# Interleaved query projections, a narrower last sampling tile and moved maxima in a four-layer image network

## The chip, the cores and the metric

The kernel runs on one core of one Trainium2 chip, as one launch. The metric is the device time of that launch in microseconds (us). A core has a matmul engine (TensorE; PE in the profile, its weight loads PEld), a vector engine (VectorE; DVE), a scalar engine (ScalarE; ACT), GpSimd (POOL) and a queue that issues transfers (SP). Each takes its own list of instructions in order, and they wait for each other by semaphores. All arithmetic here is in 32-bit floats.

## The reference

Two images of 512 channels and 64 x 64 pixels go through four layers, each of the form `x = x + layer(groupnorm(x))`. Layer 0 is an attention over local and pooled keys, layer 3 a linear attention. The change is in layer 1 and in the passage to layer 2. Cut to these:

```python
def gn(v, G=32): ...                                   # mean and variance over groups of 16 channels

def layer1(x):                                         # deformable attention
    q = einsum('oc,bchw->bohw', w_q, x)                # 512 x 4096 queries per image
    oi = q.reshape(b * 8, 64, 64, 64)                  # 8 heads of 64 channels
    off = tanh(w_off2 @ gelu(oi[:, :, ::4, ::4] * w_off1 + b_off1)) * 4.0
    grid = (16 x 16 grid points + off), scaled to the image
    kv_feats = grid_sample_bilinear(oi, grid)          # 256 points per head, sampled from q
    k, v = split(w_kv @ kv_feats)
    out = softmax((q * 64 ** -0.5) @ k) @ v            # per head, 4096 queries, 256 keys
    return w_out @ out + b_out

def layer2(x):                                         # mixture of maximum pools
    s = relu(w2 @ relu(w1 @ mean(x) + b1) + b2)        # one number per channel
    pools = [maxpool_same(x, k) for k in (1, 3, 5, 7, 9, 11, 13)]
    lower = clip(floor(s), 0, 5)
    return (s - lower) * pools[lower + 1] + (lower + 1 - s) * pools[lower] + x
```

The maximum pools are made from each other: a 3 x 3 maximum of the 3 x 3 maximum is the 5 x 5 one, and so on. The first (3 x 3) is the "maxima" of this document.

## The kernel before, in words

An image lies in on-chip memory as a tile `X` of 128 partitions x 4 chunks x 4096 pixels (a chunk is 128 channels); a second one, `Y`, holds the queries and later the pools. The pixels are cut into 8 blocks of 512 (8 rows), and each block into 4 tiles of 128 pixels. The whole program runs twice, once per image. A scheduler orders each engine's instructions when the program is built, by the order of the source, by what is ready in its own model and by hand-written restrictions such as `issue_after`; on the chip that order is fixed.

**Queries and sampling** (`query_and_sample`). `query(blk)` makes one block's queries: for each of 4 chunks, 4 matmuls of 128 x 512 (line 134) into a bank of PSUM, then a ScalarE eviction into `Y` (line 1264), and after the four a VectorE maximum over the block (line 1267). Sampling is a matmul: for each pixel tile `t`, ScalarE and VectorE make the interpolation weights of 128 pixels against the grid points of 8 heads (lines 1297 to 1299, tile `wt`, two buffers); the matmul engine turns the tile's queries so that pixels lie on partitions (4 transposes, line 1302), ScalarE copies them out (line 1305, `q_tok`, two buffers), and 8 matmuls (line 1308), one per head, add into four accumulator banks `acc`. Only grid points near the pixels can have a weight: `keys_near(t)` gives the range of grid rows, 5 to 9 of 16. The first and the last tile take all 16 rows (256 columns), and they open and close the accumulation. The outer loop makes `query(blk + 1)` and then the four tiles of `blk`; the last block has no query to make. Then line 1310 copies `acc` into `feats`, and keys and values (lines 1064 and 1070) are made from that.

**Attention and the maxima** (`layer1`). A pipelined loop over 32 steps (block, chunk): line 1440 scores, 1443 exponentials (ScalarE), 1446 their sums over two key halves (GpSimd), 1455 weighted values, 1457 eviction; per block 1465 and 1471 inverse sums (VectorE reciprocal), 1479 and 1482 division, and, some steps later, one output chunk per step: `add_output`, 4 matmuls (line 1195), a VectorE eviction into `X` (line 1198) and statistics (line 1200). When a block's output is complete, `maxima_across` (lines 1132 and 1134 on VectorE, 1131 and 1133 on ScalarE for the two halo rows and the two edge columns) takes the maximum over three columns into `rows3`, a buffer of ten rows per chunk, and `maxima_down` (lines 1145 and 1146, and 1148 for the image's last row) that over three rows, into `Y`. Blocks 0 to 6 do this for four chunks at once (2048 elements per instruction). The last block does `maxima_across` chunk by chunk, `maxima_down` for chunk 0 next, and for chunks 1 to 3 after the mixture.

**The mixture** (`pool_mixture`). After the last block's statistics (line 1114, one per chunk) a chain of small matmuls and vector operations gives the group norm and the mixture's weights per channel, from line 1157 to line 1188. Line 1187 gives the weights; the instruction returned is line 1188, and `issue_after` holds everything under it behind that instruction.

**Layer 2** (`pool_chunk`). Per chunk of 128 channels, 7 weighted sources are added up in the 8 PSUM banks as matmuls with a diagonal matrix (line 1356, 8 per source; the diagonals are made on ScalarE, line 1361, in two buffers). Sources 0 and 1 are `X` and the maxima; each of the other five is made from the one before by two VectorE maxima over a whole image chunk (line 698), with edge copies on ScalarE (line 699). Then ScalarE evicts the chunk and squares it for statistics (lines 1398 and 1402).

Of the kernel before, what the change touches and what calls it, by code (L numbers as in the profile page):

```python
# [12 lines left out]
ALU = mybir.AluOpType  # L13
# [5 lines left out]
KC = C // P  # L19
# [3 lines left out]
NB = N // TB  # L23
# [3 lines left out]
NK = 256  # L27
# [23 lines left out]
def in_turn(*gens):  # L51


    gens = list(gens)
    while gens:
        gens = [g for g in gens if next(g, gens) is not gens]
# [877 lines left out]
class Net(General):  # L934
# [102 lines left out]
    def layer1(self, X, Y, d):  # L1037

        tc, nc, vec = self.tc, self.nc, self.vec
        with tc.tile_pool(name="l1", bufs=1) as sp:  # L1040
            wkv = sp.tile([P, KC, 2 * C], F32, name="wkv1")
            nc.sync.dma_start(wkv, d["w_kv1"].rearrange("(kc p) o -> p kc o", p=P))
            wq = sp.tile([P, KC, C], F32, name="wq1")
            feats = sp.tile([P, KC, NK], F32, name="feats")
            bq = sp.tile([P, KC], F32, name="bq1")
            with tc.tile_pool(name="l1a", bufs=1) as wp, \
                    tc.tile_pool(name="l1p", bufs=4, space=PSUM) as pp, \
                    tc.tile_pool(name="l1k", bufs=1, space=PSUM) as ppk:
                grid = wp.tile([P, 2, NK], F32, name="grid")
                nc.sync.dma_start(grid, d["grid"])  # L1050
                top = sp.tile([P, KC, NB], F32, name="top_q")
                self.query_and_sample(X, Y, wq, bq, grid, feats, top, wp, pp, ppk)
            self.ahead = ExitStack()
            dp = self.ahead.enter_context(tc.tile_pool(name="diags", bufs=1, side="right"))
            self.diags = cycle([dp.tile([P, P], F32, name=f"diag{i}") for i in range(2)])
            with tc.tile_pool(name="l1c", bufs=1) as late:

                keys = late.tile([P, KC, NK], F32, name="keys")
                vals = late.tile([P, 2, C], F32, name="vals")
                with tc.tile_pool(name="l1q", bufs=4, space=PSUM) as pp:  # L1060
                    for oc in range(KC):
                        ps = pp.tile([P, TB], F32, name="mm")
                        for kc in range(KC):
                            nc.tensor.matmul(ps[:, :NK], wkv[:, kc, oc * P:(oc + 1) * P],
                                             feats[:, kc, :], start=(kc == 0), stop=(kc == KC - 1))
                        nc.scalar.mul(keys[:, oc, :], ps[:, :NK], HD ** -0.5)
                    for t in range(2):
                        ps = pp.tile([P, TB], F32, name="mm")
                        for kc in range(KC):
                            nc.tensor.matmul(ps, feats[:, kc, t * P:(t + 1) * P], wkv[:, kc, C:],  # L1070
                                             start=(kc == 0), stop=(kc == KC - 1))
                        nc.vector.tensor_copy(vals[:, t, :], ps)
                    self.product_bound(top, keys, sp, pp)
                with tc.tile_pool(name="l1b", bufs=2) as wp, \
                        tc.tile_pool(name="l1s", bufs=6, space=PSUM) as pp, \
                        tc.tile_pool(name="l1o", bufs=2, space=PSUM) as ppo:
                    st = wp.tile([P, KC, NB, 6], F32, name="gn_st1", bufs=1)
                    w1 = wp.tile([P, KC, 32], F32, name="w1", bufs=1)
                    nc.sync.dma_start(w1, d["w1"].rearrange("(kc p) e -> p kc e", p=P))
                    w2 = wp.tile([32, C], F32, name="w2", bufs=1)  # L1080
                    nc.sync.dma_start(w2, d["w2"])
                    wo = wp.tile([P, KC, C], F32, name="wo1", bufs=1)
                    nc.sync.dma_start(wo, d["w_out1"].rearrange("(kc p) o -> p kc o", p=P))
                    steps = [(blk, cc) for blk in range(NB) for cc in range(KC)]
                    part = lambda blk, cc=slice(0, KC): Y[:, cc, blk * TB:(blk + 1) * TB]
                    flat = lambda a: a.rearrange("p k o -> p (k o)")
                    probs, totals, later = {}, {}, []
                    rows3 = flat(wkv)[:, :KC * 10 * W].rearrange("p (k y x) -> p k y x", k=KC, x=W)
                    ring = cycle([a[:, n:n + TB] for a, lo, hi in (
                        (flat(wq), 0, KC), (flat(wkv), 5, 8), (flat(feats), 0, 2),  # L1090
                        (wp.tile([P, 3 * TB], F32, name="totals", bufs=1), 0, 3))
                        for n in range(lo * TB, hi * TB, TB)]).__next__
                    for i in range(len(steps) + 4 + KC):
                        if i < len(steps):
                            blk, cc = steps[i]
                            probs[i], totals[i] = self.exponentials(part(blk, cc), keys[:, cc, :],
                                                                    ring, wp, pp)
                        if 1 <= i <= len(steps):
                            blk, cc = steps[i - 1]
                            self.attended(part(blk, cc), probs.pop(i - 1),  # L1100
                                          vals[:, :, cc * P:(cc + 1) * P], ppo)
                        at = lambda n: i >= n and (i - n) % KC == KC - 1 and (i - n) // KC
                        if (blk := at(1)) is not False and blk < NB:
                            r = self.inverse_sums([totals.pop(KC * blk + n) for n in range(KC)], wp,
                                                  pp)
                        if (blk := at(2)) is not False and blk < NB:
                            self.divided(part(blk), r, pp)
                        if (blk := at(3)) is not False and blk < NB:
                            later += [(blk, oc) for oc in range(KC)]
                        if later:  # L1110
                            blk, oc = later.pop(0)
                            self.add_output(X, wo, part(blk), blk, oc, st, pp)
                            if blk == NB - 1:
                                nc.vector.bn_aggr(self.mv[:, oc, :],
                                                  st[:, oc].rearrange("p b s -> p (b s)"))
                                self.maxima_across(X, blk, rows3, slice(oc, oc + 1))
                            elif oc == KC - 1:
                                self.maxima_across(X, blk, rows3, slice(0, KC))
                                self.maxima_down(Y, blk, rows3, slice(0, KC))
                    self.maxima_down(Y, NB - 1, rows3, slice(0, 1))  # L1120
                    with tc.issue_after(self.pool_mixture(w1, w2, wp, pp)):
                        self.maxima_down(Y, NB - 1, rows3, slice(1, KC))

    def maxima_across(self, X, blk, h, ks):

# [24 lines left out]
    def pool_mixture(self, w1, w2, sp, pp):  # L1150

        nc, vec, mv = self.nc, self.vec, self.mv
        c0, d0, wts = self.mix[:, 7], self.mix[:, 8], self.mix[:, :7]
        new = lambda name, n=1: sp.tile([P, n, KC], F32, name=f"pool_{name}", bufs=1)
        nmean, cent, var, rstd = (new(n)[:, 0] for n in ("nmean", "cent", "var", "rstd"))
# [3 lines left out]
        nc.vector.tensor_tensor(cent, mv[:, :, 0], ps[:, :KC], ALU.subtract)  # L1159
        nc.vector.tensor_tensor(var, cent, cent, ALU.mult)  # L1160
        nc.vector.tensor_tensor(var, var, mv[:, :, 1], ALU.add)
        ps = pp.tile([P, TB], F32, name="mm")
        nc.tensor.matmul(ps[:, :KC], self.grp, var, start=True, stop=True)
        nc.vector.tensor_scalar(var, ps[:, :KC], 1e-5, None, ALU.add)
# [20 lines left out]
        nc.vector.tensor_tensor(up, up, down, ALU.min)  # L1185
        nc.vector.tensor_scalar(up[:, :5], up[:, :5], 0.0, None, ALU.max)
        nc.vector.tensor_tensor(wts, up, bcast(rstd, 1, 7), ALU.mult)
        return nc.vector.scalar_tensor_tensor(c0, wts[:, 0], 1.0, rstd, ALU.add, ALU.add).ins

    def add_output(self, X, w, att, blk, oc, st, pp):  # L1190

# [57 lines left out]
    def query_and_sample(self, X, Y, wq, bq, grid, feats, top, wp, pp, ppk):  # L1249
# [3 lines left out]
        nc = self.nc  # L1253
# [31 lines left out]
            nc.gpsimd.tensor_copy(wq[:, kc], w[:, kc])  # L1285
        in_turn(self.grid_steps(banks, bq, grid, ycoord, hatx, wp, pp), query(0))
        for blk in range(NB):
            if blk + 1 < NB:
                in_turn(query(blk + 1))
            for t in range(blk * NT, (blk + 1) * NT):  # L1290

                near = self.keys_near(t) if 0 < t < n_t - 1 else slice(0, 16)
                some = lambda a: a.rearrange("p g (i j) -> p g i j", j=16)[:, :, :, near]
                wt = wp.tile([P, NH, NK], F32, name="wt", bufs=2)
                nw = NK // 16 * (near.stop - near.start)
# [10 lines left out]
                for g in range(NH):  # L1306
                    cc, lo = g // 2, (g % 2) * HD
                    nc.tensor.matmul(some(acc[:, :, :NK])[lo:lo + HD, cc], q[:, g * HD:(g + 1) * HD],
                                     wt[:, g], start=(t == 0), stop=(t == n_t - 1))
        nc.vector.tensor_copy(feats, acc[:, :, :NK])  # L1310

    def keys_near(self, t):

# [1496 lines left out]
```

## Time and profile before

| what | us |
|---|---|
| median of three runs | 5074.23 (5073.88 to 5079.57) |
| the profiled execution | 5069.52 |
| span of that execution, first to last instruction | 5067.7 |
| mean granted matmul clock | 0.984 of full |
| PE idle ahead of L1308 and L1064 at the end of the sampling, first image | 3.54 and 1.32 |
| PE idle ahead of L1157, both images | 7.26 each |
| L698, one maximum over an image chunk | 4.29 |
| L1356, the products of one source after the clock has risen | 6.86 from one to the next |

A line of the timeline gives the start in us from the span's start, the duration, the engine, the line of the kernel, the operation, output and inputs with shapes, and how many records were merged; a bracket gives the engine's idle time before, and who ended it. One 128 x 512 matmul of 32-bit floats leaves two records. Busy time of the engines in five stretches of the first image (us, then busy time with the number of records; the last columns are the matmul clock granted, the share of the transfer engines and GB/s):

```profile
core 0: us, PE busy (x) PEld busy (x) DVE busy (x) ACT busy (x) POOL busy (x), PEclk, DMA share, GB/s
1188.90:1222.90 34.00, 25.75 (x189) 15.82 (x187) 18.25 (x18) 14.44 (x19) 0.00 (x0) 0.90 0.01 2
1471.00:1498.20 27.20, 27.20 (x84) 10.53 (x82) 22.78 (x24) 3.31 (x11) 2.50 (x2) 1.00 0.00 0
1498.20:1514.40 16.20, 3.65 (x21) 3.28 (x20) 11.27 (x32) 1.56 (x6) 1.02 (x1) 0.62 0.00 2
1514.40:1568.60 54.20, 50.99 (x113) 22.18 (x114) 52.88 (x15) 13.47 (x40) 0.00 (x0) 0.96 0.11 39
1568.60:1715.00 146.40, 145.28 (x341) 63.91 (x339) 130.47 (x64) 49.08 (x135) 0.85 (x1) 1.00 0.00 0
```

The first stretch is the end of the sampling, the second the last block of the attention, the third the mixture, the fourth layer 2's first chunk, the fifth its other chunks. The fourth is the one in which VectorE is busier than the matmul engine.

### The profile page before, as it was taken

The numbers are of one execution on the slowest core, as the hardware profiler recorded it, in microseconds if no ns is written. First come the engines' busy times: TensorE is split into PE (matmuls) and PEld (weight loads), VectorE is DVE, ScalarE is ACT, GpSimd is POOL, SyncE is SP. The second block draws the span as 40 slices with busy tenths as digits, with TensorE's granted clock in tenths as the row PEclk, the third lists the DMA queues.
The fourth block names the chain that finished last, engine by engine and source line by source line (L and its number), as shares of the span: only waits on it lengthen the run. The fifth ranks groups of instructions, "written<-read, shape, count | busy, mean of one in ns | idle before, by whom it ended". The sixth has DMA issues, their size and how long they took to land. (4 is left out here: it accounts for less than half of the span.)

```text
span 5067.7 us, 48015 instructions
## 1 busy us (share of the span) xinstructions
PE 4822.0 (95%) x17027; PEld 1989.3 (39%) x17027; DVE 3069.5 (61%) x4010; ACT 1818.0 (36%) x3479; POOL 1848.2 (36%) x1218
## 2 busy tenths in 40 slices
PE   7999999999999999999999999999999999999998
PEld 3423332554334444433344233335543344444333
DVE  4266777754679533477732677777536794334776
ACT  1245555334323233321112555552443232333221
POOL 0035666501320145454500456664013201454554
PEclk9999999999999999999999999999999999999999
DMA  3035556600000000211110355565000000000111
GB/s 152 3 82 141 149 146 176 166 19 10 1 3 14 2 1 1 71 55 46 63 65 3 96 139 150 147 178 148 19 10 1 17 1 1 1 1 24 40 45 44
DMA packets 124172, 307.72 MB, mean 61 GB/s; under 512 B 20818, under 2 KB 33618, under 8 KB 122388
## 3 DMA queue, kind: packets, MB, share of 16 engines
q1 hardware_dynamic: 123924, 304.58, 20.8%
q8 instruction: 136, 2.23, 0.2%
q14 instruction: 112, 0.92, 0.1%
HBM read 256.01 MB, written 48.50 MB: 60 GB/s over the span
## 5 line engine op out<-in xcount | busy, mean ns | idle before, releaser
L134 PE MATMUL mm<-big,w 128*128 128x512 f32 x2496 | 1179.5, 616 | 32.3 <-DVE big L2404 9.5
L134 PEld LDWEIGHTS mm<-big,w 128*128 128x128 f32 x2496 | 458.5, 193 | 716.9 <-issue 558.8
L2613 POOL TENSOR_TENSOR late<-late,big 128x1024 f32<-128x1024 f32 x194 | 459.9, 2371 | 228.8 <-DVE big L2608 199.9
L2447 DVE TENSOR_TENSOR prods<-qs,big 128x1024 f32<-128x1024 f32 (+1 forms) x216 | 335.4, 1570 | 66.4 <-PE tap L2474 56.2
L1643 POOL TENSOR_TENSOR big<-big 128x512 f32<-128x512 f32 x224 | 277.6, 1272 | 219.3 <-ACT big L1634 219.3
L2608 DVE TENSOR_TENSOR big<-big,mm 128x512 f32<-128x512 f32 x388 | 254.6, 681 | 114.7 <-ACT mm L2600 113.3
L2600 ACT COPY mm<-big 128x512 f32<-128x512 f32 x432 | 247.4, 596 | 123.7 <-DMA big<-rows 78.2
L1634 ACT ACTIVATE big<-mm,ed 128x256 f32<-128x256 f32 x512 | 193.6, 489 | 233.1 <-DVE top L1630 200.4
L2518 POOL TENSOR_TENSOR late<-late 128x512 f32<-128x512 f32 x92 | 115.4, 1275 | 439.2 <-ACT late L2503 415.3
L2613 POOL TENSOR_TENSOR late<-late,tap 128x1024 f32<-128x1024 f32 x94 | 221.9, 2361 | 106.5 <-DVE tap L2608 93.6
L1446 POOL TENSOR_TENSOR wq<-prob 128x512 f32<-128x512 f32 x48 | 70.8, 1497 | 501.9 <-ACT prob L1443 501.9
L1898 PE MATMUL mm<-k,w 128*128 128x512 f32 x512 | 238.4, 609 | 12.3 <-DVE k L1891 7.3
L1630 DVE TENSOR_REDUCE top<-mm 128x1 f32<-128x512 f32 x256 | 159.0, 683 | 148.2 <-PE mm L1561 148.2
L1608 PE MATMUL mm<-w,big 128*128 128x512 f32 x512 | 235.3, 603 | 0.0
L134 PE MATMUL mm<-big,wq 128*128 128x512 f32 x512 | 232.4, 603 | 2.7 <-ACT off_t L1223 2.7
L1195 PE MATMUL mm<-big,wo 128*128 128x512 f32 x512 | 234.7, 604 | 0.0
L1356 PE MATMUL acc<-big,diag 128*128 128x512 f32 x512 | 227.3, 601 | 4.6 <-ACT diag L1361 4.6
L973 POOL TENSOR_TENSOR group_stats<-group_stats,cst 128x1 f32<-128x1 f32 (+1 forms) x20 | 12.1, 621 | 560.3 <-DVE group_stats L972 500.1
L1888 DVE RECIPROCAL psD<-psD 128x512 f32<-128x512 f32 x64 | 215.1, 3361 | 1.9
L134 PE MATMUL mm<-big,big 128*128 128x512 f32 x464 | 201.7, 594 | 0.5 <-DVE b_sr L1011 0.5
L2474 PE MATMUL tap<-prods,cst 128*32 128x512 f32 x1152 | 193.1, 604 | 4.8 <-DVE prods L2447 4.3
L1443 ACT ACTIVATE prob<-mm 128x512 f32<-128x512 f32 x256 | 133.0, 603 | 171.4 <-PE mm L1440 171.1
(419 smaller groups left out, 8152.4 us busy)
## 6 DMA issues: line engine op xcount, KB each, us to landing
big<-rows SPq DMA_DIRECT2D x432, 256.0 KB, 4.2
tap<-rows SPq DMA_DIRECT2D x208, 256.0 KB, 4.1
yd<-late SPq DMA_DIRECT2D x32, 512.0 KB, 3.0
lost_all<-lost SPq DMA_DIRECT2D x128, 128.0 KB, 3.0
out<-big SPq DMA_DIRECT2D x64, 256.0 KB, 2.0
big<-in_W_kv SPq DMA_DIRECT2D x8, 1024.0 KB, 10.1
rows<-late SPq DMA_DIRECT2D x64, 128.0 KB, 3.3
big<-in_x SPq DMA_DIRECT2D x32, 256.0 KB, 3.8
```

The costliest lines, as they stand in the source:

```text
L134: self.nc.tensor.matmul(ps, w[:, kc, :], X[:, kc, blk * TB:(blk + 1) * TB], start=(kc == 0), stop=(kc == KC - 1))
L1195: nc.tensor.matmul(ps, w[:, kc, oc * P:(oc + 1) * P], att[:, kc, :], start=(kc == 0), stop=(kc == KC - 1))
L1356: nc.tensor.matmul(accs[b], dg, src[:, b * TB:(b + 1) * TB], start=(j == 0), stop=(j == 6))
L1608: nc.tensor.matmul(ps, X[:, kc, lo:lo + P], wv[:, kc, :], start=(kc == 0), stop=(kc == KC - 1))
L1634: nc.scalar.activation(f[:, t, :], pS[h][i][:, t % 2, :], AF.Exp, bias=ed[:, t, 2 * cc + h:2 * cc + h + 1])
L1643: nc.gpsimd.tensor_tensor(a, a, part, ALU.add)
L1888: nc.vector.reciprocal(psD, psD)
L1898: nc.tensor.matmul(ps, self.wo[:, kc, oc * P:(oc + 1) * P], qs[:, kc, :], start=(kc == 0), stop=(kc == KC - 1))
L2447: self.nc.vector.tensor_tensor(self.pair(u, k)[:, :n].rearrange("p k (y x) -> p k y x", x=W), bcast(qs.rearrange("p (y x) -> p y x", x=W), ...
L2600: nc.scalar.copy(ps, part)
L2608: nc.vector.tensor_tensor(part.rearrange("p (y x) -> p y x", x=W), self.vx[:, y:y + self.UY // 2, dx:dx + W], ps.rearrange("p (y x) -> p y ...
L2613: nc.gpsimd.tensor_tensor(out, out, t, ALU.add)
```

## The change

Three things. The queries of the last block are no longer made in one go before the tiles of the block before it: one chunk's projection is taken ahead of each of that block's four tiles (`ahead` is the generator of `query`, and `next` takes one step). The last sampling tile takes only its near rows (80 columns), and the accumulator is copied chunk by chunk. And the maxima of the last two blocks are split: for chunks 0 and 1 of block 6 they are written per chunk, for chunk 0 of block 7 after the first step of `pool_mixture`, which is now a generator in two steps, and all others under the `issue_after` of the mixture's last instruction.

```diff
@@ layer1 @@
                                 nc.vector.bn_aggr(self.mv[:, oc, :],
                                                   st[:, oc].rearrange("p b s -> p (b s)"))
-                                self.maxima_across(X, blk, rows3, slice(oc, oc + 1))
-                            elif oc == KC - 1:
+                                if oc < 2:
+                                    self.maxima_across(X, NB - 2, rows3, slice(oc, oc + 1))
+                                    self.maxima_down(Y, NB - 2, rows3, slice(oc, oc + 1))
+                            elif oc == KC - 1 and blk < NB - 2:
                                 self.maxima_across(X, blk, rows3, slice(0, KC))
                                 self.maxima_down(Y, blk, rows3, slice(0, KC))
+                    mixture = self.pool_mixture(w1, w2, wp, pp)
+                    next(mixture)
+                    self.maxima_across(X, NB - 1, rows3, slice(0, 1))
                     self.maxima_down(Y, NB - 1, rows3, slice(0, 1))
-                    with tc.issue_after(self.pool_mixture(w1, w2, wp, pp)):
-                        self.maxima_down(Y, NB - 1, rows3, slice(1, KC))
+                    with tc.issue_after(next(mixture)):
+                        self.maxima_across(X, NB - 1, rows3, slice(1, 2))
+                        self.maxima_down(Y, NB - 1, rows3, slice(1, 2))
+                        for blk in (NB - 2, NB - 1):
+                            self.maxima_across(X, blk, rows3, slice(2, KC))
+                            self.maxima_down(Y, blk, rows3, slice(2, KC))
@@ pool_mixture @@
         nc.vector.tensor_tensor(var, var, mv[:, :, 1], ALU.add)
+        yield
         ps = pp.tile([P, TB], F32, name="mm")
...
-        return nc.vector.scalar_tensor_tensor(c0, wts[:, 0], 1.0, rstd, ALU.add, ALU.add).ins
+        yield nc.vector.scalar_tensor_tensor(c0, wts[:, 0], 1.0, rstd, ALU.add, ALU.add).ins
@@ query_and_sample @@
         for blk in range(NB):
-            if blk + 1 < NB:
-                in_turn(query(blk + 1))
+            ahead = query(blk + 1) if blk + 1 < NB else iter(())
+            if blk < NB - 2:
+                in_turn(ahead)
             for t in range(blk * NT, (blk + 1) * NT):
-
-                near = self.keys_near(t) if 0 < t < n_t - 1 else slice(0, 16)
+                next(ahead, None)
+
+                near = self.keys_near(t) if t else slice(0, 16)
...
-        nc.vector.tensor_copy(feats, acc[:, :, :NK])
+            for _ in ahead:
+                pass
+        for cc in range(KC):
+            nc.vector.tensor_copy(feats[:, cc], acc[:, cc, :NK])
```

The order in which the changed program was built differs from the one before only in these stretches, once per image; on GpSimd and the transfer queue it is the same. On VectorE it stands as follows from block 6's first output on (numbers in brackets are block and chunk): output (6,0), across (6,0), output (6,1), across (6,1), reciprocals, output (6,2), four divisions, down (6,0), down (6,1), outputs (6,3) and (7,0), across (7,0), outputs (7,1) and (7,2), down (7,0), output (7,3), the mixture, then across (7,1) and (6,2-3) and down for both, across and down (7,2-3), and layer 2's first maximum. ("Output" is the eviction with its statistics.) On the matmul engine only the sampling's order differs: products of the last query chunk stand before, between and after the transposes of tiles 24 to 27.

## The prediction

> **What bounds the kernel now.** I read the page's table of busy time first: the matmul engine is busy for 95% of the span, so only the seams where it waits can give time back. The line shows how little room there is.
>
> ```profile
> PE 4822.0 (95%) x17027; PEld 1989.3 (39%) x17027; DVE 3069.5 (61%) x4010; ACT 1818.0 (36%) x3479; POOL 1848.2 (36%) x1218
> ```
>
> Then the timeline around the two places that the change touches, in the first image; the second image repeats both within 0.5 us. First the end of the sampling (start, duration, engine, line, operation, idle before and releaser):
>
> ```profile
> 1188.94 11.43 PE L134 MATMUL mm<-big,wq 128*128 128x512 f32 x26
> ...
> 1200.20 1.36 PE L1302 MATMUL mm<-cst,big 128*128 128x128 f32 x11
> ...
> 1212.14 2.00 ACT L1297 ACTIVATE wt<-ycoord,yneg 128x2048 f32<-128x2048 f32 x1
> ...
> 1214.17 1.23 DVE L1298 TENSOR_SCALAR wt<-wt 128x2048 f32<-128x2048 f32 x1 [0.87 <-ACT wt L1297]
> 1215.43 2.29 DVE L1299 TENSOR_TENSOR wt<-wt,hatx 128x2048 f32<-128x2048 f32 x1
> ...
> 1217.87 3.68 PE L1308 MATMUL acc<-wt,q_tok 128*64 128x256 f32 x16 [3.54 <-DVE wt L1299]
> ...
> 1222.87 7.17 PE L1064 MATMUL mm<-feats,wkv 128*128 128x256 f32 x32 [1.32 <-DVE feats L1310]
> ```
>
> From 1188.94 the matmul engine does 13 projection products without a break (two records each), and only then the last eight tiles. These run at the pace of a loop of ScalarE, VectorE and matmul with two weight buffers, and the last, full-width tile costs 2.00 + 1.23 + 2.29 + 3.68 us in a row. Second, the end of layer 1:
>
> ```profile
> 1502.62 0.74 DVE L1198 SCALAR_TENSOR_TENSOR big<-mm,vec,big 128x512 f32<-128x512 f32 x1
> ...
> 1505.06 0.36 DVE L1114 BATCH_NORM_AGGREGATE channels_mv<-gn_st 128x2 f32<-128x48 f32 x1
> ...
> 1505.48 0.59 PE L1157 MATMUL mm<-channels_mv,cst 128*128 128x4 f32 x2 [7.26 <-DVE channels_mv L1114]
> ...
> 1513.69 0.16 DVE L1188 SCALAR_TENSOR_TENSOR pool_mix<-pool_mix,pool_rstd 128x4 f32<-128x4 f32 x1
> ...
> 1517.55 4.29 DVE L698 TENSOR_TENSOR pool_h<-big 128x3968 f32<-128x3968 f32 x1
> ```
>
> The last product of L1195 ends at 1498.2, but its eviction L1198 starts at 1502.62, because VectorE is behind with maxima. The mixture then takes until 1513.69, with every engine nearly idle. Third, the matmul engine alone in layer 2:
>
> ```profile
> 1552.82 7.11 PE L1356 MATMUL acc<-pool,diag 128*128 128x512 f32 x16 [1.45 <-DVE pool L698]
> 1561.64 7.11 PE L1356 MATMUL acc<-pool,diag 128*128 128x512 f32 x16 [1.72 <-DVE pool L698]
> ```
>
> This is the line that decides. At the end of layer 2's first chunk the matmul engine already waits for VectorE's pools: VectorE, not the mixture, bounds this stretch.
>
> [...]two GpSimd sums (L1446) take 2.50 us alone and 5.23 beside L1134, which then takes 3.17 instead of 2.28. [...]Here the first products of L1356 after the mixture's gap run at 0.85 us a record instead of 0.43, for 4.3 us; the idle 3.54 us ahead of L1308 above did not slow it. [...]
>
> **The change, sampling.** The built order puts the last block's 16 products between tiles 24 to 27, and the last tile has 80 columns, not 256. The orders part after 1188.94. On the matmul engine the rest then is: 13 products at 0.86 = 11.2; 32 transposes at 0.138 (the slope from 5 records in 0.77 to 16 in 2.29) = 4.4; tile products of 128, 128, 112, 112, 112, 96, 96 and 80 columns at some 1.0, 0.9 and 0.8 by their rows = 7.25; 0.2 at each of three changes from projection to tile products (1187.81 less 1186.76, minus one product) = 0.6. Waits: tiles 24 to 28 cost 0.1, since ScalarE's evictions (L1264, 0.69) and copies (L1305, 0.57) fit inside the neighbouring tile's stretch. Tiles 29 to 31 still close the loop: products end, L1297 (0.94, 0.82 for 80 columns), L1298 and L1299 (0.55 and 0.96; 0.48 and 0.82), which leaves 0.6 + 0.65 + 0.95 = 2.2, including the 2.29 us reduction L1267 that now stands before tile 29 on VectorE. The accumulator copy, in four pieces, lets the keys start after the first: 0.5. Sum 26.25, so L1064 starts at 1215.2 instead of 1222.87: **−7.7 us per image.** Bounds: −8.8 if half of the three waits go, −6.5 if each of the four interleaved tiles shows 0.3 more. Nothing moves on the DMA queues; the loads behind L1310 (SP) start earlier with it, and they are needed some 30 us later.
>
> **The change, maxima.** Four parts.
>
> *Ahead of the reciprocals.* The across-maxima of block 6, chunks 0 and 1 (four operations of 0.67), move into VectorE's idle 0.97 and 2.30 us before L1471. They fit with 0.2 to 0.6 us over, if GpSimd's two sums at 1471.46 don't collide. [...]each holds back one VectorE operation by about 0.9 (L1134's excess), and L1471 starts 0.9 late. The matmul engine waits for L1471 directly and everything behind follows. Bounds 0 and 0.9; I take 0.4. ScalarE's small copies now stand between the last exponentials; they delay the last by 0.6, and its user is the fourth matmul of L1455, 1.4 us after the first, so this is hidden.
>
> *Up to the statistics.* VectorE has, from 1479.82: two evictions with their statistics, four divisions, and four single-chunk down-maxima, done at 1487.6. The last down-maximum of block 7, chunk 0, waits only for the first matmul of the last product (it overwrites its operand), ready at 1495.7. VectorE is thus idle when the last product ends, and L1198 starts at 1498.25, with statistics at 1499.03 and aggregate at 1499.76 against 1505.06: 5.3 earlier. L1146 and L1148 no longer stand before L1159: 0.3. The mixture, unchanged, ends **5.6 us earlier.**
>
> *After the mixture.* Before: 1.75 + 0.35 + 1.75 = 3.85 us ahead of L698. After: 14 operations. By the rows (512 elements 0.68, 1536 at 1.75, so 1024 at 1.21; 0.09 of overlap between independent neighbours) they take 7.1 us down to block 6's maxima, then 0.5 for a wait on ScalarE's halo copy (L1131), then 5.1 for block 7: 12.7. L698 starts at 1508.2 + 12.7 = 1520.9, against 1517.55: **+3.3.**
>
> *Layer 2.* L1356's first two weights start at 1508.9 and end at 1525.2; the first pool is ready two L698 later, at 1529.6. So 4.3 us of idle, then 1.9 at each of the next four (a pool costs 8.79 by the spacing of L698, its products 6.86): 11.9 in all against 3.2 before, so the 5.6 us won at the start are spent and some 3 more. The last pool's products start at 1564.9, not 1561.64. A cold clock after the 4.3 us costs 2.1 at most and is absorbed, since the next pool is later. From there to 1715 the matmul engine is busy for 145.3 of 146.4 us, so nothing recovers it. Sum **+3.7 per image.**
>
> Both images: 2 × (−7.7 + 3.7) = **−8.0 us**. The span goes from 5067.7 to 5059.7, the profiled execution from 5069.52 to 5061.5. The median of the three runs lies 4.7 above that execution; from 5074.23 I forecast 5066.2.
>
> **Rivals.** *The debt hides.* VectorE's extra 3.3 us is caught up, so only the sampling counts: 2 × −7.7 = −15.4, 5058.8. For it: VectorE has slack of 9 to 12 us in chunk 1. Against: the waits of 1.45 and 1.72 lie before that slack.
> *Both gains.* The mixture's 5.6 us come through as well: 2 × −13.3 = −26.6, 5047.6. Only the waits shown above speak against it, and they would have to be misread.
> *Half the sampling.* Only the narrow last tile pays (about 4 us), since the interleaving gives back what it fills: 2 × (−4 + 3.7), 5073.6.
> *ScalarE closes the loop (slower).* In tiles 24 to 27 the next |y| activation (1.04), the eviction (0.69) and the copy (0.57) stand in one in-order queue, each waiting for another matmul. If they run one after the other in the matmul engine's way, 2.4 us with latency, four tiles cost 9.6: the sampling loses 1.9 and the sum is 2 × (1.9 + 3.7) = +11.2, 5085.4. It decides from 1.0 us a tile, where gain and debt are equal. Against: 2.3 us of projections lie between.
>
> **How the numbers follow.** A change of 0.2% is 10.1 us, about what a measurement of this kernel can tell from none; the forecast of −8.0 lies inside. Chances: forecast 0.63, debt hidden 0.15, both 0.05, half 0.11, slower 0.06. The forecast's own spread (the bounds above, some 3 us, and as much between runs) puts 0.14 of its 0.63 beyond −10.1. Faster 0.34, same 0.60, slower 0.06. The range, 5058.5 to 5072.5, takes in the hidden debt and most of the half gain.
>
> **What would show it.** L1064's counterpart starting 7 to 8 us earlier after the shared products; no idle over 0.3 us before tile products 24 to 28; the mixture's first matmul about 2 us after the last product instead of 7.3; then VectorE's fourteen maxima ahead of the first L698, and five waits of L1356 for a pool, near 4.3 and four times 1.9. If these waits stay near 3 us in all, the debt was hidden[...].

## The result, and the profile after

| kernel | median, us | lowest to highest | runs |
|---|---|---|---|
| before | 5074.55 | 5068.96 to 5081.50 | 20 |
| changed | 5064.74 | 5056.07 to 5074.27 | 20 |

The ratio is 0.9982 (95% interval 0.9976 to 0.9988): 9.8 us faster by the medians, 6.1 to 12.2 by the interval. The forecast was 5066.2. The profiled execution of the changed kernel took 5062.35 us, its span 5060.5 instead of 5067.7.

The matmul engine alone, changed kernel, at the end of the sampling; the last line is the same place in the second image (start, duration, engine, line, operation, idle before and releaser; lines from the maxima on are 9 to 15 higher than before):

```profile
1210.99 0.88 PE L1320 MATMUL acc<-wt,q_tok 128*64 128x96 f32 x16 [0.82 <-DVE wt L1311]
1212.45 0.88 PE L1320 MATMUL acc<-wt,q_tok 128*64 128x96 f32 x16 [0.58 <-DVE wt L1311]
1214.30 0.77 PE L1320 MATMUL acc<-wt,q_tok 128*64 128x80 f32 x16 [0.96 <-DVE wt L1311]
1215.59 8.73 PE L1064 MATMUL mm<-feats,wkv 128*128 128x256 f32 x32 [0.52 <-DVE feats L1325]
...
3733.72 7.17 PE L1064 MATMUL mm<-feats,wkv 128*128 128x256 f32 x32 [0.52 <-DVE feats L1325]
```

From 1186 to 1210.99 no product waits; only the last three tiles do, 0.82 + 0.58 + 0.96 us. The keys (L1064) start at 1215.59, not 1222.87. But in the first image their 32 records take 8.73 us, in the second 7.17: the first time the granted clock was 0.50 from 1215.35 to 1218.77, the second time 1.00 throughout (the last section has both).

VectorE and GpSimd just ahead of the last reciprocals, from the view of all engines:

```profile
1465.61 2.93 POOL L1461 TENSOR_TENSOR wq<-prob 128x512 f32<-128x512 f32 x2 [5.70 <-ACT wkv L1142]
...
1465.70 1.72 DVE L1141 TENSOR_TENSOR wkv<-big 128x496 f32<-128x496 f32 x1
...
1467.51 1.58 DVE L1143 TENSOR_TENSOR wkv<-wkv,big 128x512 f32<-128x512 f32 x1
...
1470.40 0.66 DVE L1141 TENSOR_TENSOR wkv<-big 128x496 f32<-128x496 f32 x1
...
1471.16 0.69 DVE L1143 TENSOR_TENSOR wkv<-wkv,big 128x512 f32<-128x512 f32 x1
```

The two across-maxima of block 6, chunk 0, take 1.72 and 1.58 us beside GpSimd's two sums; the same two operations for chunk 1, after the sums, take 0.66 and 0.69. The matmul engine again, from there to layer 2's second chunk:

```profile
1475.18 1.14 PE L1494 MATMUL mm<-recip,cst 2*128 2x512 f32 x8 [1.13 <-DVE recip L1486]
1476.26 17.43 PE L1205 MATMUL mm<-big,wo 128*128 128x512 f32 x40
1495.67 0.39 PE L1166 MATMUL mm<-channels_mv,cst 128*128 128x4 f32 x2 [1.98 <-DVE channels_mv L1114]
...
1503.93 16.45 PE L1371 MATMUL acc<-big,diag 128*128 128x512 f32 x32 [2.30 <-ACT diag L1376]
1525.02 16.14 PE L1371 MATMUL acc<-pool,diag 128*128 128x512 f32 x32 [4.63 <-DVE pool L698]
1542.63 7.11 PE L1371 MATMUL acc<-pool,diag 128*128 128x512 f32 x16 [1.48 <-DVE pool L698]
1551.45 7.11 PE L1371 MATMUL acc<-pool,diag 128*128 128x512 f32 x16 [1.72 <-DVE pool L698]
1560.27 7.11 PE L1371 MATMUL acc<-pool,diag 128*128 128x512 f32 x16 [1.72 <-DVE pool L698]
1567.21 20.76 PE L1371 MATMUL acc<-big,diag 128*128 128x512 f32 x48
```

The reciprocals now hold up the division's matmuls by 1.13. After the last product the mixture follows 1.98 us later, not 7.26. Then layer 2 pays: its first pool comes 4.63 us late, three others 1.48 to 1.72. VectorE shows why, between the mixture's last operation and the first maximum over a whole chunk (the maxima lie in the gap of the fence):

```profile
1503.18 0.16 DVE L1198 SCALAR_TENSOR_TENSOR pool_mix<-pool_mix,pool_rstd 128x4 f32<-128x4 f32 x1
...
1516.18 4.29 DVE L698 TENSOR_TENSOR pool_h<-big 128x3968 f32<-128x3968 f32 x1
```

From 1503.27 to 1516.18, 12.9 us, VectorE is now at maxima there (0.53 of it a wait for a halo copy), where 3.85 us of work stood before.

**A ledger.** The matmul engine has the same number of records (17027) in every kernel here, and the same order outside the sampling, so there record n of one profile can be set against record n of another. The table gives, for the first and second image, how much later (+) or earlier (-) than in the profile of the kernel before: the keys start, counted from the tiles ahead of the seam; the keys last; the division's matmuls start, counted from the product before the reciprocals; the mixture starts, counted from the division; and the product that follows layer 2's first chunk and the one that follows its last, both counted from the product before the reciprocals. The first row is the changed kernel, the others are the experiments that follow.

| kernel | keys start | keys last | division | mixture | first chunk ends | last chunk ends |
|---|---|---|---|---|---|---|
| changed | -7.91, -7.59 | +1.55, 0 | +1.19, +1.19 | -5.28, -3.58 | +4.36, +6.60 | +4.36, +6.64 |
| e1_sampling | -7.89, -7.57 | +1.69, +1.65 | 0, 0 | 0, 0 | 0, 0 | 0, 0 |
| e2_maxima | -0.31, +0.32 | 0, +1.42 | +1.19, +1.20 | -5.28, -5.28 | +4.34, +4.72 | +4.36, +4.76 |
| e3_narrow | -5.40, -5.16 | +2.16, +2.25 | 0, 0 | 0, 0 | 0, 0 | 0, 0 |
| e7_interleave | -1.65, -1.33 | +1.80, +2.06 | 0, 0 | 0, 0 | 0, 0 | 0, +0.1 |
| e5_behind | -7.90, -7.58 | 0, 0 | 0, 0 | -5.28, -5.28 | +3.16, +3.51 | +3.17, +3.54 |
| e4_deferred | -7.89, -7.58 | 0, 0 | 0, 0 | -5.28, -5.28 | -7.58, -7.79 | +0.10, -0.64 |
| e6_spread | -7.90, -7.59 | 0, 0 | 0, 0 | -5.28, -5.28 | -7.80, -7.81 | -1.04, -1.01 |
| e8_edges | -7.89, -7.58 | 0, +1.60 | 0, 0 | -5.28, -5.28 | -7.81, -6.62 | -5.79, -4.60 |

In the changed kernel's second image the last products of layer 1 ran 1.70 us longer at half clock (0.50 granted from 3993.80 to 3997.21), which is why its mixture gains 3.58 there and its chunks end later; e5, e4, e6 and e8 show 5.28 in both images.

### The profile page after: what moved, and what is told of

Read it like the earlier page. It is cut to its first block, busy times and chain, and to the rows that moved or that the text cites. A ratio compares the mean times of both kernels' runs of the same rounds, so it can differ in the third digit from the quotient of the medians.

```text
span 5060.5 us, 48047 instructions
## 1 busy us (share of the span) xinstructions
PE 4826.2 (95%) x17027; PEld 1989.5 (39%) x17027; DVE 3074.4 (61%) x4034; ACT 1817.4 (36%) x3483; POOL 1849.3 (37%) x1218
```

## The experiments

Theory A: the sampling brings the whole gain; the maxima part costs, first because two of its operations take 1.95 us longer together beside GpSimd's sums (1.72 and 1.58 us, not 0.66 and 0.69), then because VectorE's work ahead of layer 2's first pool grew by more than the mixture came forward. The rivals: both parts bring half each; or VectorE's extra work is caught up later, so that the maxima part costs nothing.

**e1_sampling.** The two parts apart: `query_and_sample` of the changed kernel, everything else as before.

```diff
-            if blk + 1 < NB:
-                in_turn(query(blk + 1))
+            ahead = query(blk + 1) if blk + 1 < NB else iter(())
+            if blk < NB - 2:
+                in_turn(ahead)
...
+                next(ahead, None)
-                near = self.keys_near(t) if 0 < t < n_t - 1 else slice(0, 16)
+                near = self.keys_near(t) if t else slice(0, 16)
...
```

> The sampling part alone; the maxima stay as in the kernel before. Theory A (the sampling gains 7.3 to 7.6 us per image, the maxima part costs 1.2 through the late reciprocals and 3.2 through the later pools): keys' first matmul some 7.4 us earlier per image, nothing else changed, 14.8 us faster than the kernel before, near 5059.7. Theory B (each part brings about half of the measured 9.8 us): near 5069.6. [...]

Measured 5058.90 against 5075.56 (ratio 0.9965, 0.9956 to 0.9975): 16.7 us faster, near Theory A and far from B. The sampling alone is faster than the whole change.

**e2_maxima.** The other half: `layer1` and `pool_mixture` of the changed kernel, the sampling as before.

```diff
-                                self.maxima_across(X, blk, rows3, slice(oc, oc + 1))
-                            elif oc == KC - 1:
+                                if oc < 2:
+                                    self.maxima_across(X, NB - 2, rows3, slice(oc, oc + 1))
+                                    self.maxima_down(Y, NB - 2, rows3, slice(oc, oc + 1))
+                            elif oc == KC - 1 and blk < NB - 2:
...
+                    mixture = self.pool_mixture(w1, w2, wp, pp)
+                    next(mixture)
...
```

> The maxima part alone; the sampling stays as in the kernel before. Theory A: mixture 5.3 us earlier after the last product, but the reciprocals of the last block 1.2 late and layer 2's first chunk ending 3.2 later against the last product, so 2 x 4.4 = 8.8 us slower than the kernel before, near 5083. Theory B (each part brings half): near 5069.6. Theory C (VectorE's extra work is caught up later): no change within 2 us, near 5074.5.

Measured 5082.45 against 5075.56 (ratio 1.0015, 1.0006 to 1.0023). Slower, as Theory A has it; B and C fall. In the ledger the first chunk ends 4.34 and 4.72 us later and the last chunk 4.36 and 4.76: what the first chunk lost, the others did not give back.

**e3_narrow** and **e7_interleave.** The sampling's two edits apart, on the kernel before. The narrow tile:

```diff
-                near = self.keys_near(t) if 0 < t < n_t - 1 else slice(0, 16)
+                near = self.keys_near(t) if t else slice(0, 16)
```

> The kernel before with the last sampling tile's near rows (80 columns) as its only edit: no interleaved projections, one copy of the accumulator. Theory A: the last tile's chain shrinks from 2.00 + 1.23 + 2.29 + 3.68 to some 0.8 + 0.5 + 0.8 + 0.8 us and no longer ends late; keys' first matmul about 6.3 us earlier per image, 12.6 us faster in all, near 5062: most of the sampling's gain without the interleaving. Theory B, that of the forecast's third rival (the narrow tile gives about 4 us and the interleaving the rest): 8 us faster, near 5066.5.

Measured 5069.17 against 5075.56 (0.9986, 0.9978 to 0.9994): 6.4 us, where Theory A has 12.6, outside the interval, and Theory B 8. The interleaving, with the copy in four pieces, is e1_sampling with this line put back:

```diff
-                near = self.keys_near(t) if t else slice(0, 16)
+                near = self.keys_near(t) if 0 < t < n_t - 1 else slice(0, 16)
```

> The interleaved projections and the copy in four pieces alone, the last sampling tile at its full 256 columns, maxima as in the kernel before. Theory A (the last tile's chain was most of the sampling's loss, 5.4 us of 7.4 in the narrow-tile run's trace): keys' first matmul 1.8 us earlier per image, 3.6 faster than the kernel before, near 5072. Theory B (the interleaving is worth as much as the sum of both parts less the narrow tile alone by the measured times, 16.7 - 6.4 = 10 us): near 5065.

Measured 5074.89 against 5074.98 (0.9998, 0.9989 to 1.0006): no change; the interval has room for A's 3.6 us, not for B's 10. The starts of the keys came out better than the times (5.40 and 5.16 us for the narrow tile, where 6.3 was expected; 1.65 and 1.33 for the interleaving), and they add up to 7.1 and 6.5 of the 7.9 and 7.6 of both. The matmul engine's view of e3_narrow shows what came between:

```profile
1213.32 0.99 PE L1308 MATMUL acc<-wt,q_tok 128*64 128x112 f32 x16 [1.41 <-DVE wt L1299]
1214.78 1.18 PE L1308 MATMUL acc<-wt,q_tok 128*64 128x96 f32 x16 [0.48 <-DVE wt L1299]
1217.02 2.71 PE L1308 MATMUL acc<-wt,q_tok 128*64 128x96 f32 x32 [1.05 <-DVE wt L1299]
1221.04 9.34 PE L1064 MATMUL mm<-feats,wkv 128*128 128x256 f32 x32 [1.32 <-DVE feats L1310]
```

The keys take 9.34 us instead of 7.17. The products of the last two tiles are slow too, 2.71 us for 32 records that take 0.88 + 0.77 in the changed kernel: the granted clock was 0.50 from 1215.5 to 1218.5 and 0.80 in the mean from 1206 to 1231. That is the 1 us by which the start fell short of what was expected, and the keys lose 2.2 more. Each edit alone so loses about 2 us per image again; with both, in six profiles, the keys lost between 0 and 1.7. The measured times of e3 and e7 (6.4 and 0.1 us) add up to 10.2 less than the 16.7 of e1. The ledger has 6.9 of that: 2.0 in the starts of both images and 4.9 in the lengths of the keys. The other 3.3 lie within the intervals, which are some 4 to 5 us wide either way.

**e5_behind.** The across-maxima without GpSimd's sums beside them: those of block 6, chunks 0 and 1, are queued behind the reciprocals, when GpSimd has nothing to do. For Theory A the 1.95 us more beside the sums made the reciprocals late, by 1.13 to 1.2 us.

```diff
-                                    self.maxima_across(X, NB - 2, rows3, slice(oc, oc + 1))
+                                    with tc.issue_after(self.inverted):
+                                        self.maxima_across(X, NB - 2, rows3, slice(oc, oc + 1))
...
-            nc.vector.reciprocal(r[:, half], psD[:, half])
+            self.inverted = nc.vector.reciprocal(r[:, half], psD[:, half]).ins
```

> The changed kernel with the across-maxima of block 6, chunks 0 and 1, queued behind the last block's reciprocals, where GpSimd has no sums to make. Theory A [...]: each of the four takes about 0.67, the wait of 1.13 ahead of the division's matmuls is gone, the mixture starts no later after the last product; 2 x 1.2 us faster than the changed kernel, near 5062.3. Theory B (the operations are only moved: what the reciprocals win, the last statistics lose): mixture 1 us or more later after the last product, total as the changed kernel, near 5064.7. The time alone can't tell 2.4 us; the waits in the trace do.

Measured 5062.87 against 5074.98 (0.9974, 0.9965 to 0.9983). The time can't tell it from the changed kernel; the matmul engine's view can:

```profile
1473.99 1.14 PE L1495 MATMUL mm<-recip,cst 2*128 2x512 f32 x8
1475.07 17.43 PE L1206 MATMUL mm<-big,wo 128*128 128x512 f32 x40
1494.48 0.39 PE L1167 MATMUL mm<-channels_mv,cst 128*128 128x4 f32 x2 [1.98 <-DVE channels_mv L1114]
```

The wait of 1.13 ahead of L1495 is gone, and the mixture stands 19.41 us after the products' start (1494.48 less 1475.07), exactly as in the changed kernel (1495.67 less 1476.26). Behind the reciprocals the four operations take 0.61 to 0.69 us each. So they cost nothing where they went: Theory A.

**e4_deferred.** The main test of Theory A: leave only chunk 0's maxima ahead of the first pool, and make those of chunks 1 to 3 where each chunk begins.

```diff
-                                if oc < 2:
+                                if oc == 0:
...
-                    with tc.issue_after(next(mixture)):
-                        self.maxima_across(X, NB - 1, rows3, slice(1, 2))
...
+                    next(mixture)
...
+    def late_maxima(self, X, Y, cc, h):
...
+        n = 2 * TB // W
+        x, out, own = image(X[:, cc, :])[:, W - n - 2:], image(Y[:, cc, :]), h[:, :n + 2]
+        nc.vector.tensor_tensor(own[:, :, 1:W - 1], x[:, :, :W - 2], x[:, :, 2:], ALU.max)
+        nc.scalar.copy(own[:, :, 0:W:W - 1], x[:, :, 1:W - 1:W - 3])
+        nc.vector.tensor_tensor(own, own, x, ALU.max)
...
@@ pool_chunk @@
         h = image(self.scratch)
+        if cc:
+            self.late_maxima(X, Y, cc, h)
```

> The changed kernel, but ahead of layer 2's first pool VectorE makes only chunk 0's maxima; those of chunks 1 to 3 for the last two blocks are made at the start of each chunk of layer 2 (18 rows at once, in the pools' scratch). Theory A (VectorE's 13 us ahead of the first pool set the end of chunk 0): first pool right behind the mixture, chunk 0's products without a wait, ending about 12 us earlier per image than in the changed kernel; chunks 1 to 3 then carry 5.4 us of VectorE work each and give back some 5 in waits; the reciprocals no longer late (1.2). In all 2 x 8 = 16 us faster than the changed kernel, near 5048.5. Theory B (the debt comes back whole in chunks 1 to 3, as VectorE is as busy as the matmul engine there): only the 2 x 1.2 of the reciprocals, near 5062.

Measured 5052.19 against 5075.56 (five runs; 0.9959, 0.9946 to 0.9973). Between the two theories. The division is no longer late, with one pair of across-maxima ahead of the reciprocals instead of two. The first chunk behaves as Theory A says (it ends 7.6 and 7.8 us earlier than before, 12 to 14 earlier than in the changed kernel), but 7.7 and 7.2 of that are given back by the end of the last chunk. The matmul engine's waits in that stretch:

```profile
1553.21 7.11 PE L1382 MATMUL acc<-pool,diag 128*128 128x512 f32 x16 [1.57 <-DVE pool L698]
...
1603.13 7.11 PE L1382 MATMUL acc<-pool,diag 128*128 128x512 f32 x16 [1.61 <-DVE pool L698]
...
1653.07 25.13 PE L1382 MATMUL acc<-big,diag 128*128 128x512 f32 x58 [1.64 <-DVE big L698]
...
1685.39 6.25 PE L1382 MATMUL acc<-big,diag 128*128 128x512 f32 x14 [0.95 <-DVE group_stats L967]
...
1694.18 5.16 PE L1382 MATMUL acc<-pool,diag 128*128 128x512 f32 x8 [2.43 <-DVE group_stats L972]
```

**e6_spread.** Is it VectorE's load that gives it back? Part of the deferred work goes into gaps that VectorE has earlier.

```diff
+                                    with tc.issue_after(self.last_div):
-                                    self.maxima_across(X, NB - 2, rows3, slice(oc, oc + 1))
-                                    self.maxima_down(Y, NB - 2, rows3, slice(oc, oc + 1))
+                                        self.maxima_across(X, NB - 2, rows3, slice(oc, oc + 1))
+                                        self.maxima_down(Y, NB - 2, rows3, slice(oc, oc + 1))
...
-        nc.vector.scalar_tensor_tensor(d0, nmean, 2.0, rstd, ALU.mult, ALU.mult)
+        yield nc.vector.scalar_tensor_tensor(d0, nmean, 2.0, rstd, ALU.mult, ALU.mult).ins
...
+                    with tc.issue_after(next(mixture)):
+                        self.maxima_across(X, NB - 2, rows3, slice(2, 3))
+                        self.maxima_down(Y, NB - 2, rows3, slice(2, 3))
...
+        n = (2 if cc == KC - 1 else 1) * TB // W
```

> As the deferred version, but less is deferred: block 6's maxima of chunks 0 and 1 stand behind the last divisions, in VectorE's gaps of the last outputs, those of chunk 2 in the 2.8 us in which VectorE waits for the mixture's small matmuls; in layer 2, chunks 1 and 2 make only block 7's maxima (10 rows, some 3.2 us), chunk 3 both blocks' (5.4 us). Theory A (VectorE's work in layer 2 is what the deferred version still pays for: waits of 1.6 us in each chunk and 3.4 us ahead of the last statistics): the waits of chunks 1 and 2 go, those of the statistics shrink; 3 to 5 us per image faster than the deferred version (5052.2), near 5044. Theory B (the waits that it fills were not free: the mixture ends later by as much): the mixture 2 us or more later after the last product, near 5052 or above.

Measured 5054.98 against 5074.98 (five runs; 0.9952, 0.9938 to 0.9965); the times can't tell it from e4_deferred. The gaps were free: the mixture stands where it stood. But the waits did not go, so this form of Theory A falls. The matmul engine:

```profile
1602.11 7.11 PE L1387 MATMUL acc<-pool,diag 128*128 128x512 f32 x16 [1.62 <-DVE pool L698]
...
1652.04 25.13 PE L1387 MATMUL acc<-big,diag 128*128 128x512 f32 x58 [1.62 <-DVE big L698]
```

At the start of chunk 1 VectorE had 2.1 us less to do (3.2 instead of 5.4), and yet the second maximum started as late as in e4_deferred, 10.27 us after the last pool's products of chunk 0:

```profile
1555.38 4.29 DVE L698 TENSOR_TENSOR pool_h<-big 128x3968 f32<-128x3968 f32 x1
1562.46 4.29 DVE L698 TENSOR_TENSOR big<-pool_h 128x3968 f32<-128x3968 f32 x1 [2.79 <-ACT pool_h L699]
```

It waits 2.79 us for an edge copy on ScalarE, which stands there behind the evictions of the chunk before (the last of them in the fence):

```profile
1559.63 0.70 ACT L1429 ACTIVATE big<-acc,pool_mix 128x512 f32<-128x512 f32 x1
...
1561.29 0.73 ACT L1433 ACTIVATE pool_sq<-big,pool_shift 128x512 f32<-128x512 f32 x1
...
1561.99 0.43 ACT L699 COPY pool_h<-big 128x128 f32<-128x128 f32 x1
```

Nothing that the copy needs was later than the maximum before it, which ended at 1559.67; ScalarE came to the copy at 1561.99, and the next maximum started 0.04 us after the copy's end. The evictions in turn wait for the matmul engine: the last starts at 1559.63, 0.34 us after the chunk's products end (1552.19 + 7.10). So each chunk's end set VectorE's start into the next, however little VectorE had to do.

**e8_edges.** Take that copy out of ScalarE's queue: e6_spread with this edit.

```diff
...
+                edges = nc.vector.tensor_copy if cc and j == 2 else nc.scalar.copy
-                self.spread_max(h, last, 2)
-                self.spread_max(image(flat), h, 1)
+                self.spread_max(h, last, 2, edges)
+                self.spread_max(image(flat), h, 1, edges)
```

> As the spread version, but the edge copies of the first two maxima of chunks 1 to 3 in layer 2 are made by VectorE (four small operations of some 0.2 us a chunk) and not by ScalarE. Theory A (in the deferred and the spread version the second maximum of each chunk waits for an edge copy that stands in ScalarE's queue behind the evictions of the chunk before, so the matmul engine's own end of a chunk sets VectorE's start into the next): VectorE's waits of 2.79 and 2.78 us ahead of the second maximum go, the matmul engine's waits of 1.6 us in chunks 1 and 2 go, those for the last statistics shrink; layer 2 ends 3 to 5 us earlier per image than in the spread version against the mixture, in all 6 to 10 us faster than it, near 5045. Theory B (VectorE's total work is the bound, the edge copy only happened to come last): another wait takes its place, the matmul engine's waits in chunks 1 and 2 stay within 0.5 us, time as the spread version, 5050 to 5055.

Measured 5044.53 against 5077.35 (five runs; ratio 0.9938, 0.9925 to 0.9952). VectorE makes the copy in 0.30 us (and a second one per chunk, two in all and not four) and goes on at once:

```profile
1555.13 4.29 DVE L698 TENSOR_TENSOR pool_h<-big 128x3968 f32<-128x3968 f32 x1
1559.34 0.30 DVE L699 COPY pool_h<-big 128x128 f32<-128x128 f32 x1
1559.68 4.29 DVE L698 TENSOR_TENSOR big<-pool_h 128x3968 f32<-128x3968 f32 x1
```

And the matmul engine runs through both ends of chunks that cost 1.6 us each:

```profile
1593.21 7.03 PE L1387 MATMUL acc<-big,diag 128*128 128x512 f32 x16
1600.08 7.03 PE L1387 MATMUL acc<-pool,diag 128*128 128x512 f32 x16
...
1641.28 7.03 PE L1387 MATMUL acc<-pool,diag 128*128 128x512 f32 x16
1648.15 25.05 PE L1387 MATMUL acc<-big,diag 128*128 128x512 f32 x58
```

In the ledger the last chunk ends 4.8 and 3.6 us earlier than in e6_spread, where 3 to 5 were expected: Theory A. This version is some 20 us faster than the changed kernel by the medians, and its median is the lowest here. From the first chunk's end to the last's it still loses 2.0 us against the kernel before; the same view shows waits for statistics of 1.24, 0.79 and 0.47 us in the last chunk, where the kernel before has the 0.79 alone.

## Why the prediction was right, step by step

**Net and sign.** Forecast -8.0 us, measured -9.8, with the two parts of opposite sign as forecast: e1_sampling -16.7 (forecast of that part -15.4), e2_maxima +6.9 (forecast +7.4). The debt that hides and the gain from both fall with e2_maxima, the ScalarE loop with the tiles 24 to 28, which have no wait at all.

**Sampling, -7.7 per image.** Measured -7.91 and -7.59. The three remaining waits, 0.6 + 0.65 + 0.95, came out as 0.82 + 0.58 + 0.96, the copy's wait of 0.5 as 0.52. What the forecast read wrongly is the clock: "the idle 3.54 us ahead of L1308 above did not slow it". In the profile of before the last tile's 16 products ran at half clock (this view gives from and to, the length, busy time and records of the matmul engine, its weight loads, VectorE, ScalarE and GpSimd, then the granted clock, the transfers' share and GB/s):

```profile
1217.87:1221.55 3.68, 3.68 (x16) 1.88 (x16) 0.00 (x0) 0.00 (x0) 0.00 (x0) 0.50 0.02 4
```

The tiles of 96 to 144 columns grow by 0.11 us for 16 columns, from 0.88 to 1.20; by that, an estimate, 256 columns at full clock take some 2 us and not 3.68. The sum of the forecast is not hurt, since it starts from measured times and gives the new tile 0.8 us (measured 0.77). But it does not count half clock on other products: in the changed kernel's first image the keys had 0.50 from 1215.59 to 1218.77 and took 1.55 us longer. The rival "half the sampling" had 4 us per image from the narrow tile and nothing from the interleaving; e1_sampling, 16.7 us faster and not 8, rules it out. By itself the narrow tile starts the keys 5.3 us earlier and keeps 3 of them.

**Ahead of the reciprocals, 0.4, bounds 0 and 0.9.** The step that failed in size: "each holds back one VectorE operation by about 0.9 (L1134's excess), and L1471 starts 0.9 late" added only one of two delays. Beside GpSimd's two sums (1465.61 to 1468.54) the two operations took 1.72 - 0.66 and 1.58 - 0.69, together 1.95 us longer, of which the division's matmuls waited 1.19; the other 0.76 went into the room that the gap had (forecast 0.2 to 0.6). The forecast's own terms, twice 0.9 less that room, would have given 1.2 to 1.6. In e4_deferred, with one pair of these operations (0.66 and 1.57), the reciprocals still wait 1.10 us for the matmul engine: one pair with one lengthened operation fits, two pairs with two do not. Without the GpSimd sums beside them, in e5_behind, the four take 0.61 to 0.69 us and the wait is gone. What makes them longer beside the sums is not shown.

**Mixture 5.6 us earlier.** The forecast had the last statistics 5.3 earlier and the mixture's end 5.6. Its start came 5.28 earlier against the division and follows the last product after 1.98 (forecast about 2). Its end came 5.98 earlier: 1503.18 less 1475.18 in the changed kernel, 1513.69 less 1479.71 before, by this line of the profile of before:

```profile
1479.71 1.14 PE L1479 MATMUL mm<-recip,cst 2*128 2x512 f32 x8
```

In the table of five stretches before the change, the third, the mixture, is the other one in which VectorE is busier than the matmul engine (11.27 us against 3.65): its maxima held the statistics back. They held the mixture's own operations back as well: L1159 was ready near 1506.27, when L1158 on ScalarE ended (1506.10 + 0.17), and started at 1506.61, behind the unrelated L1148 (1506.48) on VectorE.

**Fourteen operations, 12.7 us.** Measured 12.9 (1503.27 to 1516.18). The first pool's products were forecast to wait 4.3, then 1.9 four times; measured 4.63, then nothing, 1.48, 1.72 and 1.72. The second wait is missing because the products ahead of it ran at half clock after the 4.63 (0.50 granted from 1522.55 to 1529.38), took 16.14 us where two sources at full clock take 6.86 + 7.11, and so ended late themselves: this was absorbed, as forecast. The forecast's 2.1 for it is an estimate: 4.3 us at 0.85 a record instead of 0.43, as L1356 ran after the mixture in the profile of before. The last pool's products stand 3.2 us later against the division than before; forecast 3.3. "Nothing recovers it" holds to 0.05 us in e2_maxima.

**What the sum leaves, and luck.** 2 x (-7.75 + 1.19 + 3.2) is -6.7, and the row of the changed kernel, with its losses to the clock, sums to -3.0; the measured -9.8 has -6.1 at the end of its interval. So the terms are shown one by one, but that -8.0 came so near -9.8 is in part luck: the late reciprocals, and the half clock that the forecast did not count, do not show in the measured time, which is lower than either sum. Stretches without an edit move single profiles by as much: the nine other profiles reach the tiles ahead of the first seam 0.6 to 7.1 us later than the profile of before, and pass from the first image's layer 2 to the second image's seam between 7.9 us faster and 1.7 slower. The medians of most kernels here lie some 2 to 9 us below what their ledgers sum to, and the profile of before, against which the ledger is made, was itself an execution 5 us below its median. What makes up that difference in the medians stays open.

## What to carry to other kernels

When a serial stretch between two matmul phases is shortened by pushing work behind it, look at what that work stands in front of: the engine that has the least slack right after the stretch decides, not the stretch (here VectorE: 5.28 us won on the mixture, 4.63 us of wait for the first pool). Work that belongs to a later unit (here chunks 1 to 3) goes to that unit's start, and small helper copies must not stand in a queue that waits for the unit before (2.79 us at the start of chunk 1 in e6_spread). Two GpSimd operations beside two VectorE ones lengthened both here, by 1.06 and 0.89 us, so count every pair.

## What the hardware showed beyond the forecast

In the profiles of the kernel before and of the changed one the granted clock of the matmul engine is either 1.00 or 0.50, with 31 and 32 stretches at 0.50. In each profile the changes lie on a grid: the half-clock stretches start at multiples of 3.4133 us from one another, to 0.01 us (1215.35 and 1498.66 in the changed kernel are 83 steps apart, 1215.37 and 3737.82 in the one before 739), and last one to five steps (only the one at the end of the span is cut). In e3_narrow no long wait stands ahead of the slow keys: the waits before them are 1.41, 0.48, 1.05 and 1.32 us, each between busy records. What tells the cases at this seam apart is how much the engine was busy within one step of the grid. The changed kernel, first image, then the second image with the same waits of 0.82, 0.58 and 0.96 us (columns as in the view of windows above):

```profile
1211.94:1215.35 3.41, 1.66 (x32) 1.36 (x32) 1.93 (x4) 1.30 (x2) 0.00 (x0) 1.00 0.00 0
1215.35:1218.77 3.42, 3.18 (x8) 2.56 (x9) 1.18 (x4) 0.00 (x0) 0.00 (x0) 0.50 0.38 59
...
3727.58:3730.99 3.41, 2.01 (x33) 1.64 (x33) 2.85 (x5) 2.55 (x5) 0.00 (x0) 1.00 0.00 0
3730.99:3734.41 3.42, 1.94 (x31) 1.57 (x28) 2.43 (x6) 0.38 (x1) 0.00 (x0) 1.00 0.03 7
3734.41:3737.82 3.41, 3.41 (x18) 3.00 (x17) 0.25 (x1) 0.73 (x2) 0.00 (x0) 1.00 0.91 217
```

In the first image one step holds most of the waiting, the engine is busy for 1.66 of 3.41 us, and the next step, with the keys in it, runs at half clock. In the second image the waiting is spread over two steps, with 2.01 and 1.94 us busy, and the clock stays full. In the kernel before, the steps ahead of half clock were busy for 1.02 and 1.58 us (from 1211.96 and 3734.41), while those of 1.73 and 2.01 (from 1208.54 and 3730.99) were followed by full clock. Elsewhere in the two profiles steps at full clock with 1.5 to 2.6 us busy went either way (in the changed kernel 1.51 from 3375.99 and 2.45 from 2710.39 ahead of half clock, 1.59 from 334.71 and 2.27 from 2526.07 ahead of full), so this is a reading of this seam and no general threshold. The changed kernel's waits are the same in both images and fall differently on the grid: the keys lost 1.55 us in one image and nothing in the other.
